# Four graph layers on 2708 nodes: queries, keys, values and outputs of a head as one run in DRAM

## The chip, the cores and the metric

The kernel runs on one core of a Trainium2 chip. The metric is device time in microseconds (us) from the start of the program to its end. A profile is one more execution, taken by the hardware profiler. The core has TensorE (PE, with its weight loads as PEld), VectorE (DVE), ScalarE (ACT), GpSimd (POOL) and SyncE (SP), each with its own queue in program order, and 16 DMA engines. Nearly all plain DMAs of this kernel are issued from SP; gathers and scatters by index are issued from POOL.

## The reference, cut to what matters

Input are 2708 nodes with 128 features and a dense matrix `adj` of 2708 x 2708, in which about 4 entries of a row and the diagonal are not zero. Four layers each normalise x, apply a relu, and add their result to x. The change concerns layer 1, graph attention. Here h is the normalised x:

```python
q = (h @ Wq.T).reshape(d, n, heads)      # d = 128, n = 2708, heads = 8
k = (h @ Wk.T).reshape(d, n, heads)
v = (h @ Wv.T).reshape(d, n, heads)
a = einsum('dnh,dmh->dnm', q, k) * d**-0.5 + adj + adj
a = softmax(a, axis=2)
out = einsum('dnm,dmh->dnh', a, v).reshape(n, heads * d)
x = x + out @ Wo.T
```

The reshape doesn't split features into heads. h @ Wq.T has 2708 rows of 1024 numbers, which are read as one long list of 2708 * 128 groups of eight numbers. What the kernel calls head d (there are 128) is groups d*2708 to d*2708 + 2707 of that list; node n of head d comes from row (d*2708 + n) // 128 of the projection. Layer 0 before and layers 2 and 3 after use the same `adj` and are not changed.

## The kernel before, in words

**Projection** (L620 to L655). Six chunks of up to 512 nodes; for each of the three weights and each of eight elements e one matmul with 128 weight columns stationary and up to 512 columns of hT moving, 144 in all. ACT and DVE in turn copy a result to every 25th element of a tile `qkv`, which is stored to `qkv_c`, laid out [128 groups of a row][node rows][25]: 8 of q, 8 of k, 8 of v and a one. Beside this, `in_order` (L560) sorts the lists of neighbours; its 22 scatters `list_d` (L612) on POOL each wait for the one before.

**The loop over heads** (L1258 to L1321). For each of 128 heads it goes six rounds. The softmax is split: without `adj` the exponential is a polynomial, evaluated by `keys`, `queries`, `moments`, `turn` and `evaluate` for all pairs of nodes; the few pairs with an `adj` entry are corrected apart. Nodes are spread over partitions as node t*128+p on partition p, t from 0 to 21, so that the last tile t = 21 has 20 rows only. `prepare` (L787) loads four heads (a group; there are 32) from `qkv_c` to `raw`, with `from_heads` (L545), which needs one or two DMAs a head. Queries are transposed by PE (L1226), ACT copies them (`fT`, L1228), and PE multiplies (L1238).

**Beside the loop** generators are advanced by a pace of 1.5 steps a round: first `by_node` (L829) loads each group once more (`n_raw`, three buffers), ACT copies it so that eight heads of a node are adjacent (`n_kv` two buffers, `n_q` one buffer), and for every pair of groups SP stores `kv_n` in pieces of 512 bytes and `q_n` in pieces of 256 bytes. Then `sorted_rows`, then `from_neighbours` (L891), which gathers `kv_n` rows of each node's neighbours and scatters corrections to `more_n`. When these are done, two steps a round go to `normalise` (L1033) and `project_out` (L669). A group's polynomial sums were stored to `o_g` by `sums` (L821); `normalise` loads them and the corrections, adds them on POOL, divides on DVE and stores outputs to `o_c` with `to_heads` (L550). `project_out` loads a tile of nodes as [groups][nodes][8], and multiplies eight times with a stationary operand of every eighth element. Generators yield a number of rounds to wait (`LOAD, SOON = 4, 2`). `begin` and `step` (L1089, L1108) choose what is advanced.

**Order.** The whole loop is in an order written out by hand (`manual_schedule`), so each engine's queue has its instructions as the source lists them. After the loop bounds are computed (L1325 to L1366), and what is left beside it is finished. If a bound failed, dense attention would be computed by loops L1423 to L1500; on these inputs these loops run zero times.

Of the kernel before, what the change touches and what calls it, by code (L numbers as in the profile page):

```python
# [45 lines left out]
def gnn4_kernel(  # L46
# [211 lines left out]
    with ExitStack() as ph:  # L258
# [9 lines left out]
        def by_head(src, name):  # L268

            nat = ap.tile([P, KC, C], FP, name=f"{name}_nat", tag="a_nat")  # L270
            nc.sync.dma_start(nat, src.rearrange("(t p) c -> p t c", p=P))
            dst = bp.tile([P, HEAD, C], FP, name=name)
            for i0, iw in _cuts(KC, 4):
                pt = ps.tile([P, BK], FP, name="w_ps", tag="tr")
                for i in range(iw):
                    nc.tensor.transpose(pt[:, i * P : (i + 1) * P], nat[:, i0 + i], ident)
                c0, cw = i0 * P // HEAD, iw * P // HEAD
                nc.vector.tensor_copy(
                    dst[:, :, c0 : c0 + cw],
                    pt[:, : iw * P].rearrange("p (c h) -> p h c", h=HEAD),  # L280
                )
            return dst
# [35 lines left out]
        with tc.manual_schedule():  # L318
# [3 lines left out]
            wT = [by_head(w, f"wT{i}") for i, w in enumerate((wq, wk, wv))]  # L322
# [207 lines left out]
    qkv_c = dram.tile([P, N + 1, QKV], FP, name="qkv_c")  # L530
    o_c = dram.tile([P, N, HEAD], FP, name="o_c")
# [6 lines left out]
    def runs(d, t0, n=P):  # L538

        sh, r = d * N % P, d * N // P + t0  # L540
        if sh + n <= P:
            return [(0, n, sh, r)]
        return [(0, P - sh, sh, r), (P - sh, n, 0, r + 1)]

    def from_heads(eng, dst, src, d, t0, nt, n=P):  # L545

        for p0, p1, c, r in runs(d, t0, n):
            eng.dma_start(dst[p0:p1], src[c : c + p1 - p0, r : r + nt])

    def to_heads(eng, dst, src, d, t0, nt, n=P):  # L550
        for p0, p1, c, r in runs(d, t0, n):
            eng.dma_start(dst[c : c + p1 - p0, r : r + nt], src[p0:p1])
# [67 lines left out]
    with ExitStack() as ph:  # L620
# [6 lines left out]
        zero = lp.tile([P, QKV], FP, name="zero")  # L627
        nc.gpsimd.memset(zero, 0.0)
        nc.sync.dma_start(qkv_c[:, N], zero)
        with tc.manual_schedule():  # L630
            ots = [op.tile([P, BK, QKV], FP, name=f"qkv{i}") for i in range(2)]
# [4 lines left out]
            for c, (c0, cw) in enumerate(cols):  # L636
                ot = ots[c % 2]
                for i in range(3):
                    for e in range(HEAD):
                        pq = pm.tile([P, BK], FP, name="qkv_ps", tag="mm")  # L640
                        nc.tensor.matmul(
                            pq[:, :cw], wT[i][:, e], hT[:, c0 : c0 + cw], start=True, stop=True
                        )
                        scale = (C**-0.5, 1.0, 1.0)[i]
                        to = ot[:, :cw, i * HEAD + e]
                        n += 1
                        if n % 2:
                            nc.scalar.mul(to, pq[:, :cw], scale)
                        else:
                            nc.vector.tensor_scalar_mul(to, pq[:, :cw], scale)  # L650
                            next(sort, None)
                nc.sync.dma_start(qkv_c[:, c0 : c0 + cw], ot[:, :cw])
# [4 lines left out]
    def load_wo(lp, wk_pool, ps, tag):  # L657
        wo_nat = wk_pool.tile([P, HD], FP, name="wo_nat", tag=tag)
        nc.sync.dma_start(wo_nat, wo)
        wo_h = wo_nat.rearrange("p (c k) -> p k c", k=HEAD)  # L660
        woT = lp.tile([P, HEAD, C], FP, name="woT")
        for k0, kw in _cuts(HEAD, 4):
            pt = ps.tile([P, 4, C], FP, name="wo_ps", tag="tr")
            for k in range(kw):
                nc.tensor.transpose(pt[:, k], wo_h[:, k0 + k], ident)
# [3 lines left out]
    def project_out(op, tag, bank, woT, t):  # L669
        r0, sz = rows[t]  # L670
        o = op.tile([P, P, HEAD], FP, name="o_cr", tag=tag)
        nc.sync.dma_start(o[:, :sz], o_c[:, r0 : r0 + sz])
        yield LOAD
        po = bank(t)
        for k in range(HEAD):
            nc.tensor.matmul(
                po[:sz], o[:, :sz, k], woT[:, k], start=k == 0, stop=k == HEAD - 1
            )
        yield SOON
        nc.vector.tensor_tensor(x_sb[:sz, t], x_sb[:sz, t], po[:sz], ALU.add)  # L680

    LOAD, SOON = 4, 2
# [3 lines left out]
    with ExitStack() as ph:  # L686
# [100 lines left out]
        def prepare(g, got):  # L787

            raw = kp.tile([P, GRP, NT, QKV], FP, name="raw")
            for i in range(GRP):  # L790
                from_heads(nc.sync, raw[:, i], qkv_c, g * GRP + i, 0, NT)
            for _ in range(8):
                yield
            for e, at in enumerate((q_at, k_at)):
# [11 lines left out]
            nc.vector.reduce_sum(  # L806
                part, v[:, :, :NF].rearrange("p i t k -> p i k t"), axis=AX.X
            )
# [4 lines left out]
            nc.tensor.matmul(to, ones, flat, start=True, stop=not REM)  # L813
            if REM:
                nc.tensor.matmul(to, ones[:REM], v[:REM, :, NF], start=False, stop=True)
# [13 lines left out]
        def by_node():  # L829
# [3 lines left out]
            def load(j):  # L833
                raws[j] = big.tile([P, GRP, NT, QKV], FP, name="n_raw", tag="big")
                for i in range(GRP):
                    from_heads(nc.sync, raws[j][:, i], qkv_c, j * GRP + i, 0, NT)
# [4 lines left out]
            for j in range(NG):  # L841
# [8 lines left out]
                for dst, src in (  # L850
# [4 lines left out]
                    nc.scalar.copy(dst, raw[:, :, :, src].rearrange("p i t k -> p t i k"))  # L855
                    yield
                    yield
                if j % 2:
                    hs = slice((j - 1) * GRP, (j + 1) * GRP)
                    store_rows(  # L860
# [4 lines left out]
                    store_rows(  # L865
# [167 lines left out]
        def normalise(g, ring):  # L1033

            if ring == "tm":
                ro = tm.tile([P, NT, GRP, VW], FP, name="r_raw", tag="tmp")
                co = tm.tile([P, NT, GRP, VW], FP, name="r_more", tag="c_q")
            else:
                both = big.tile([P, 2, NT, GRP, VW], FP, name="r_both", tag="big")
                ro, co = both[:, 0], both[:, 1]  # L1040
            nc.sync.dma_start(ro.rearrange("p t i k -> p (t i k)"), o_g[g])
            nc.sync.dma_start(
                co.rearrange("p t i k -> p t (i k)"),
                more_n[:, g * GRP : (g + 1) * GRP].rearrange("(t p) i k -> p t (i k)", p=P),
            )
            yield LOAD
            nc.gpsimd.tensor_tensor(ro, ro, co, ALU.add)
            yield SOON
            rs = sm.tile([P, NT, GRP], FP, name="r_rs")
            on = lp.tile([P, GRP, NT, HEAD], FP, name="r_on", tag="n_kv", bufs=2)  # L1050
# [7 lines left out]
            for t0, nt, sz in ((0, NF, P), (NF, 1, REM)):  # L1058
                for i in range(GRP if sz else 0):
                    to_heads(nc.sync, o_c, on[:sz, i, t0 : t0 + nt], g * GRP + i, t0, nt, sz)  # L1060
# [18 lines left out]
        rings = {"tm": [], "big": []}  # L1079
        room = {"tm": 2, "big": 3}  # L1080
        banks = []

        def bank(t):

            if not banks:
                banks.append(ps_v.tile([P, 2, BK], FP, name="v_ps"))
            return banks[0][:, t % 2, :C]

        def begin(summed):  # L1089

            if not beside or beside[0][1] >= summed:
                return None
            i, need, norm = beside[0]
            if not norm and any(e[2] <= need for e in under_way):
                return None
            for ring in ("tm", "big") if norm else ("big",):
                if len(rings[ring]) < room[ring]:
                    beside.pop(0)
                    gen = (
                        normalise(i, ring) if norm else project_out(big, "big", bank, woT, i)  # L1100
                    )
# [50 lines left out]
        got = []  # L1152
        fks, ys, fqs, fts, pms, mws, ros = {}, {}, {}, {}, {}, {}, {}
# [40 lines left out]
        def moments(d, h, n0, n1):  # L1194
# [3 lines left out]
            for t in range(*parts[h])[n0:n1]:  # L1198
                sz, m = rows[t][1], t - parts[h][0]
                nc.tensor.matmul(  # L1200
                    pms[d][:, :P],
                    fks[d][:sz, t],
                    ys[d, h][:sz, m * VW * B_ALL : m * VW * B_ALL + P],
# [53 lines left out]

        with tc.manual_schedule():  # L1258
# [20 lines left out]
            for d in range(D):  # L1279
                asked = queries(d + 1) if d + 1 < D else iter(())  # L1280
                for c in range(NCH):
# [31 lines left out]
                    if first is None:  # L1313
                        owed = 0
                        for _ in range(2):
                            step(n, max(d // GRP - 1, 0))
                g = d // GRP
                if d % GRP == GRP - 1:
# [6 lines left out]
            nc.vector.memset(top, 0.0)  # L1325
            p2 = sm.tile([C, 2], FP, name="p2")
            for e in range(2):
                pt = ps_t.tile([P, BK], FP, name="g_tr", tag="tr")
                nc.tensor.transpose(pt[:C, :P], most2[:, e], ident)
                nc.vector.tensor_reduce(p2[:, e : e + 1], pt[:C, :P], axis=AX.X, op=ALU.max)  # L1330
            nc.vector.tensor_tensor(top[:, 0:1], p2[:, 0:1], p2[:, 1:2], ALU.mult)
            nc.vector.tensor_tensor(top[:, 1:2], p2[:, 0:1], p2[:, 1:2], ALU.max)
            nc.vector.tensor_reduce(top[:, 2:3], nval, axis=AX.XY, op=ALU.max)
            nc.vector.tensor_reduce(top[:, 3:4], nval, axis=AX.XY, op=ALU.min)
            low = sm.tile([P, 1], FP, name="low")
            nc.vector.tensor_scalar_mul(top[:, 3:4], top[:, 3:4], -1.0)
            nc.vector.tensor_reduce(low, below, axis=AX.X, op=ALU.max)
            nc.vector.tensor_tensor(top[:, 3:4], top[:, 3:4], low, ALU.max)
            nc.vector.tensor_tensor(top[:, 3:4], top[:, 3:4], full, ALU.max)
            nc.vector.tensor_reduce(low, eighth, axis=AX.X, op=ALU.max)  # L1340
            nc.vector.tensor_tensor(top[:, 3:4], top[:, 3:4], low, ALU.max)
            pt = ps_t.tile([P, BK], FP, name="g_tr", tag="tr")
            nc.tensor.transpose(pt[:4, :P], top, ident)
            t4 = sm.tile([4, 1], FP, name="top4")
            nc.vector.tensor_reduce(t4, pt[:4, :P], axis=AX.X, op=ALU.max)
# [427 lines left out]
```

## Time and profile before

| | |
|---|---|
| median of 3 runs | 3328.97 us (3327.44 to 3329.23) |
| profiled execution | 3354.19 us, its span 3352.4 us |
| PE busy | 2691.7 us, 80% of the span |
| PE weight loads | 2273.0 us, 68% |
| DVE busy | 2202.7 us, 66% |
| ACT busy | 1314.8 us, 39% |
| POOL busy | 2009.3 us, 60% |
| DMA moved | 462.08 MB, mean 138 GB/s |
| packets under 512 B, of all | 159,650 of 312,741 |
| mean granted clock of TensorE | 0.89 |

The page gives busy times over the whole span, but the kernel is a sequence of stages with different limits, so shares of the span say little; the prediction cuts it into stages. A group of instructions is shown as line, engine, operation, tiles out<-in, count, then busy time and the mean of one in ns, and after the next bar the engine's idle time ahead of them. A wait is shown as "engine line <- whom it waited for: us in total, times, longest". In a table of stretches, DMA share is the mean busy share of the 16 DMA engines, so that 0.25 is four engines' worth.

### The profile page before, as it was taken

Reading aid. Unit: us, or ns where it says so; the run is one execution under the profiler, and the core shown is the slowest. Engines: PE = TensorE matmul, PEld = TensorE weight load, DVE = VectorE, ACT = ScalarE, POOL = GpSimd, SP = SyncE. Lnnn points to the kernel's source line nnn. Section 1 sums busy time; section 2 is a strip of 40 time slices with the busy share of each in tenths; the row PEclk is TensorE's granted clock in tenths of the full one; section 3 lists DMA queues with packets and bytes.
Section 4 is the critical chain, followed back from the end, with each engine's and each line's share of the span. In section 5 each row is a group of like instructions: output and inputs, shape, how many; then the busy total and the mean of one; then the engine's idle time right before and its main releaser. Section 6 shows DMA issues by size and latency. Waiting matters only on the chain. (4 is left out here: it accounts for less than half of the span.)

```text
span 3352.4 us, 50866 instructions
## 1 busy us (share of the span) xinstructions
PE 2691.7 (80%) x17781; PEld 2273.0 (68%) x17781; DVE 2202.7 (66%) x5135; ACT 1314.8 (39%) x3127; POOL 2009.3 (60%) x2263
## 2 busy tenths in 40 slices
PE   6477884888789999999999999999888897796044
PEld 4476543777788887888888788877777886443033
DVE  3868753666678888888888788887666675213222
ACT  3485462555544444444444444444322232102010
POOL 0111115555588888888988888889656663000775
PEclk6688896999999999999999999999888999895565
DMA  3452274777743333333334333343465712541322
GB/s 113 175 227 93 76 326 128 208 214 206 211 131 114 125 125 127 128 132 128 119 138 139 126 141 125 137 143 121 94 148 143 166 48 64 193 176 56 106 83 61
DMA packets 312741, 462.08 MB, mean 138 GB/s; under 512 B 159650, under 2 KB 234404, under 8 KB 289330
## 3 DMA queue, kind: packets, MB, share of 16 engines
q1 hardware_dynamic: 280870, 289.79, 28.3%
q0 software_dynamic: 31600, 168.86, 14.7%
q8 instruction: 148, 2.42, 0.3%
q14 instruction: 123, 1.01, 0.1%
HBM read 344.89 MB, written 113.67 MB: 137 GB/s over the span
## 5 line engine op out<-in xcount | busy, mean ns | idle before, releaser
L1238 PE MATMUL g_ps<-mw,fT 128*128 128x128 f32 x5632 | 817.5, 287 | 155.2 <-ACT fT L1228 115.1
L1238 PEld LDWEIGHTS g_ps<-mw,fT 128*128 128x128 f32 x5632 | 715.4, 196 | 290.6 <-ACT fT L1228 178.4
L1228 ACT COPY fT<-f_ps 128x512 f32<-128x512 f32 (+1 forms) x768 | 420.6, 548 | 1216.7 <-PE f_ps L1226 1216.6
L1200 PE MATMUL m_ps<-y,fk 128*128 128x128 f32 (+1 forms) x5632 | 768.2, 280 | 0.0
L1200 PEld LDWEIGHTS m_ps<-y,fk 128*128 128x128 f32 (+1 forms) x5632 | 699.9, 194 | 15.4
L1150 POOL TENSOR_TENSOR y<-bk,raw 128x792 f32<-128x792 f32 x256 | 415.8, 1624 | 432.1 <-ACT y L1181 420.3
L1246 DVE TENSOR_TENSOR z<-g_ps,bq 128x324 f32<-128x324 f32 (+1 forms) x768 | 355.6, 463 | 435.0 <-PE g_ps L1238 433.6
L1226 PE MATMUL f_ps<-ident,fq 128*128 128x128 f32 x2816 | 441.6, 276 | 14.4 <-DVE v_sum L817 9.3
L1252 DVE TENSOR_REDUCE o_raw<-z 128x36 f32<-128x324 f32 (+1 forms) x768 | 355.8, 463 | 26.4
L1150 POOL TENSOR_TENSOR fk<-bk,raw 128x352 f32<-128x352 f32 (+1 forms) x384 | 357.7, 955 | 0.1
L1226 PEld LDWEIGHTS f_ps<-ident,fq 128*128 128x128 f32 x2816 | 340.2, 144 | 16.2 <-DVE v_sum L817 10.6
L1150 POOL TENSOR_TENSOR fk<-raw,bk 128x352 f32<-128x352 f32 (+1 forms) x512 | 312.6, 640 | 3.1 <-ACT bk L719 2.3
L1147 DVE TENSOR_TENSOR fq<-bq,kq_ps 128x528 f32<-128x528 f32 (+1 forms) x512 | 288.2, 605 | 0.0
L930 POOL TENSOR_TENSOR c_z<-c_kv,c_q 128x1024 f32<-128x1024 f32 (+1 forms) x121 | 284.2, 2349 | 2.2 <-DMA c_kv<-kv_n,srt 1.4
L971 PE MATMUL v_ps<-c_v,ident 128*128 128x512 f32 (+1 forms) x484 | 233.3, 605 | 15.3 <-ACT c_acc L986 15.3
L1591 POOL DMA_INDIRECT g<-gate_d,srt x121 | 120.4, 995 | 110.2 <-issue 109.0
L1147 DVE TENSOR_TENSOR fq<-kq_ps,bq 128x352 f32<-128x352 f32 (+1 forms) x512 | 171.9, 378 | 0.0
L155 POOL CAST n_fl<-n_ci 128x40 f32<-128x40 int32 (+1 forms) x22 | 4.8, 218 | 251.9 <-DVE n_ci L138 251.9
L936 DVE TENSOR_REDUCE c_c<-c_z 128x128 f32<-128x1024 f32 (+1 forms) x121 | 147.5, 1219 | 3.4 <-POOL c_z L930 3.2
L954 DVE TENSOR_TENSOR c_v<-c_kv,c_c 128x1024 f32<-128x1024 f32 (+1 forms) x121 | 146.7, 1212 | 0.0
L971 PEld LDWEIGHTS v_ps<-c_v,ident 128*128 128x128 f32 (+1 forms) x484 | 82.0, 189 | 79.1 <-issue 58.8
L915 POOL DMA_INDIRECT c_kv<-kv_n,srt x121 | 117.8, 974 | 23.1 <-issue 9.6
(290 smaller groups left out, 3714.1 us busy)
## 6 DMA issues: line engine op xcount, KB each, us to landing
a_nat<-in_adj_dram SPq DMA_DIRECT2D x34, 1354.0 KB
qkv_c<-qkv SPq DMA_DIRECT2D x5, 6400.0 KB
a<-in_adj_dram SPq DMA_DIRECT2D x21, 1354.0 KB
kv_n<-n_kv SPq DMA_DIRECT2D x16, 1344.0 KB
o_g<-o_raw SPq DMA_DIRECT2D x32, 396.0 KB
q_n<-n_q SPq DMA_DIRECT2D x16, 672.0 KB
o_cr<-o_c SPq DMA_DIRECT2D x21, 512.0 KB
r_raw<-o_g SPq DMA_DIRECT2D x22, 396.0 KB
```

Of the source, the lines that this page charges most:

```text
L930: nc.gpsimd.tensor_tensor(zs[b][:sz], kvs[b][:sz, 0, :, 0], qs[t][:sz], ALU.mult)
L936: nc.vector.reduce_sum(cs[b][:sz], zs.pop(b)[:sz], axis=AX.X)
L954: nc.vector.tensor_tensor(z[:sz], kv[:sz, 0, :, 1].rearrange("p (j c) k -> p j c k", j=2), c.rearrange("p (j c) -> p j c", j=2)[:, :, :, None]
L971: nc.tensor.matmul(accs[t][:sz, j], ident[:sz, :sz], z[:sz, j].rearrange("p c k -> p (c k)"), start=s0 == 0, stop=s0 == ROOM[t] - 1,)
L1147: nc.vector.tensor_tensor(o, x, y, ALU.mult)
L1150: nc.gpsimd.tensor_tensor(o, x, y, ALU.mult)
L1200: nc.tensor.matmul(pms[d][:, :P], fks[d][:sz, t], ys[d, h][:sz, m * VW * B_ALL : m * VW * B_ALL + P], start=t == 0, stop=t == NT - 1,)
L1226: nc.tensor.transpose(pt[:, m], fqs[d][:, t0 + m], ident)
L1228: nc.scalar.copy(fts[d, c][:, :n], pt[:, :n])
L1238: nc.tensor.matmul(pg[:, m], ft[:, m], mws[d], start=True, stop=True,)
L1246: nc.vector.tensor_tensor(z[:, :n], pg[:, :n, : B_ALL * VW].rearrange("p t (k b) -> p t k b", k=VW), bqs[d % 2][:, t0 : t0 + n, None, :B_A ...
L1252: nc.vector.reduce_sum(ros[g][:, t0 : t0 + n, i], z[:, :n], axis=AX.X,)
```

## The change

All of layer 1 uses the flat order of the list. `qkv_d` has one row of 25 numbers for each of 2708 * 128 groups, `o_d` one row of 8, so that a head is one run of rows. A head's 2708 nodes are cut into 123 runs of 22 and a rest of two: node p*22+t lies on partition p, and partition 123 holds the rest. The other partitions of two fixed `raw` buffers are set to zero once, so `moments` and the sum of v use all 128 rows of every tile. Groups, per-node data and outputs are loaded and stored by one DMA for 123 partitions and a small one for the rest.

The projection goes by 22 tiles of nodes: hT stationary, 512 weight columns moving, six matmuls a tile, 132 in all, copied in runs of eight, with a store of 12,800 bytes a partition for each tile. The output projection loads whole rows of 1024 numbers, turns them by eight PE transposes, ACT copies them in two pieces, and eight matmuls follow later. `normalise` waits one more step before its store; the last group takes its sums from SBUF rather than from `o_g`. Spacing is `LOAD, SOON = 6, 2`; three steps a round are tried, and a group may begin earlier. The bounds are computed in small steps during the last three heads.

```diff
-    qkv_c = dram.tile([P, N + 1, QKV], FP, name="qkv_c")
-    o_c = dram.tile([P, N, HEAD], FP, name="o_c")
+    qkv_d = dram.tile([N * (P + 1), QKV], FP, name="qkv_d")
+    o_d = dram.tile([N * P, HEAD], FP, name="o_d")
...
+    WHOLE = N // NT
+    LEFT = N - WHOLE * NT
...
+    def group_of(src, g):
+
+        flat = src[g * GRP * N : (g + 1) * GRP * N].rearrange("(i n) k -> i n k", n=N)
+        return (
+            flat[:, : WHOLE * NT].rearrange("i (p t) k -> p i (t k)", t=NT),
+            flat[:, WHOLE * NT :].rearrange("(o i) n k -> o i (n k)", o=1),
+        )
+
+    def load_group(eng, dst, g):
+
+        main, rest = group_of(qkv_d, g)
+        eng.dma_start(dst[:WHOLE].rearrange("p i t k -> p i (t k)"), main)
+        eng.dma_start(
+            dst[WHOLE : WHOLE + 1, :, :LEFT].rearrange("p i t k -> p i (t k)"), rest
+        )
+
+    def store_group(eng, g, src):
+
+        main, rest = group_of(o_d, g)
+        eng.dma_start(main, src[:WHOLE].rearrange("p i t k -> p i (t k)"))
...
+    def store_nodes(eng, dst, src):
+
+        eng.dma_start(
+            dst[: WHOLE * NT].rearrange("(p t) k -> p t k", t=NT), src[:WHOLE]
+        )
+        eng.dma_start(
+            dst[WHOLE * NT :].rearrange("(o t) k -> o t k", o=1),
+            src[WHOLE : WHOLE + 1, :LEFT],
+        )
...
-            for c, (c0, cw) in enumerate(cols):
-                ot = ots[c % 2]
+            for t, (r0, sz) in enumerate(rows):
+                ot = ots[t % 3]
                 for i in range(3):
-                    for e in range(HEAD):
+                    scale = (C**-0.5, 1.0, 1.0)[i]
+                    for c0 in (0, HALF):
                         pq = pm.tile([P, BK], FP, name="qkv_ps", tag="mm")
                         nc.tensor.matmul(
-                            pq[:, :cw], wT[i][:, e], hT[:, c0 : c0 + cw], start=True, stop=True
+                            pq[:sz],
+                            hT[:, r0 : r0 + sz],
+                            wT[i][:, c0 * HEAD : (c0 + HALF) * HEAD],
+                            start=True,
+                            stop=True,
                         )
...
+        pt = turn_bank()
+        for k in range(KC):
+            nc.tensor.transpose(
+                pt[:, k // 4, (k % 4) * P : (k % 4) * P + sz],
+                nat[:sz, k * P : (k + 1) * P],
+                ident[:sz, :sz],
+            )
+        for j in range(KC // 4):
+            nc.scalar.copy(
+                oT[:, 4 * j : 4 * j + 4, :sz],
+                pt[:, j].rearrange("p (k c) -> p k c", k=4)[:, :, :sz],
+            )
+        yield SOON
+        add_sums()
+        po = sum_bank()
+        for k in range(KC):
             nc.tensor.matmul(
-                po[:sz], o[:, :sz, k], woT[:, k], start=k == 0, stop=k == HEAD - 1
-            )
+                po[:sz], oT[:, k, :sz], woT[:, k], start=k == 0, stop=k == KC - 1
+            )
...
-    LOAD, SOON = 4, 2
+    LOAD, SOON = 6, 2
...
-            raw = kp.tile([P, GRP, NT, QKV], FP, name="raw")
-            for i in range(GRP):
-                from_heads(nc.sync, raw[:, i], qkv_c, g * GRP + i, 0, NT)
+            raw = raws_g[g % 2]
+            load_group(nc.sync, raw, g)
...
-                for i in range(GRP):
-                    from_heads(nc.sync, raws[j][:, i], qkv_c, j * GRP + i, 0, NT)
+                main, _ = group_of(qkv_d, j)
+                nc.sync.dma_start(raws[j][:WHOLE].rearrange("p i t k -> p i (t k)"), main)
...
-                    store_rows(
+                    store_nodes(
                         nc.sync,
                         kv_n[:, hs].rearrange("n i k -> n (i k)"),
                         kv.rearrange("p t j i e k -> p t (j i e k)"),
                     )
...
+        raws_g = [lp.tile([P, GRP, NT, QKV], FP, name=f"raw{i}") for i in range(2)]
+        for b in raws_g:
+            nc.gpsimd.memset(b, 0.0)
...
-                    fks[d][:sz, t],
-                    ys[d, h][:sz, m * VW * B_ALL : m * VW * B_ALL + P],
+                    fks[d][:, t],
+                    ys[d, h][:, m * VW * B_ALL : m * VW * B_ALL + P],
...
-                        for _ in range(2):
-                            step(n, max(d // GRP - 1, 0))
+                        for _ in range(3):
+                            step(n, max((d - 1) // GRP, 0))
+                    if d >= D - 3:
+                        next(limits, None)
                 g = d // GRP
-                if d % GRP == GRP - 1:
+                if d % GRP == GRP - 1 and g < NG - 1:
                     sums(g, ros.pop(g))
```

## The prediction

> **What bounds the kernel now.** I read the page's slices first, then cut the span into stages at the lines that begin and end them: layer 0 to 379 us, projection of queries, keys and values to 497, start-up of the attention loop to 563, the loop to 2828, its tail to 2866, layers 2 and 3. The stage table (busy time of each engine, granted clock, DMA share, GB/s):
>
> ```profile
> core 0: us, PE busy (x) PEld busy (x) DVE busy (x) ACT busy (x) POOL busy (x), PEclk, DMA share, GB/s
> 379.00:497.00 118.00, 114.12 (x293) 53.52 (x292) 79.31 (x103) 73.18 (x73) 17.10 (x19) 0.97 0.60 253
> 497.00:563.00 66.00, 12.28 (x62) 10.93 (x62) 11.72 (x41) 6.50 (x20) 27.64 (x38) 0.53 0.52 173
> 563.00:953.00 390.00, 325.07 (x2554) 305.54 (x2554) 254.11 (x613) 214.38 (x478) 224.53 (x304) 0.93 0.70 191
> 953.00:2386.00 1433.00, 1338.51 (x9664) 1154.56 (x9665) 1177.39 (x2537) 622.93 (x1677) 1246.30 (x1304) 0.99 0.37 128
> 2386.00:2828.00 442.00, 372.68 (x2712) 353.65 (x2711) 288.35 (x643) 133.78 (x346) 261.43 (x276) 0.93 0.49 114
> 2828.00:2866.00 38.00, 16.60 (x75) 14.51 (x73) 10.02 (x38) 0.00 (x0) 5.70 (x4) 0.64 0.45 119
> ```
>
> TensorE fills the projection and the loop's middle. The stage 563 to 953 is another: beside the loop, `by_node` rewrites everything per node, and DMA is at 0.70. The waits of that stage already show the loop held by a store, because ACT takes its work in order:
>
> ```profile
> ACT n_q L855 <- DMA q_n<-n_q: 31.7, 5, 8.3
> ```
>
> So I looked at how fast single transfers go there. Three narrow windows: 607.0 to 608.5, in which only the load issued at 604.3 still moves (163.3 KB, that is 76 rows of 2200 B), then a kv_n store (512 B pieces, 128 partitions), then a q_n store (256 B pieces):
>
> ```profile
> 607.00:608.50 1.50, 1.50 (x16) 1.50 (x15) 0.85 (x2) 0.77 (x2) 0.00 (x0) 1.00 0.26 100
> 609.00:613.00 4.00, 3.27 (x26) 2.79 (x25) 1.69 (x5) 2.57 (x5) 0.43 (x1) 1.00 1.03 290
> 614.00:616.80 2.80, 1.78 (x16) 1.59 (x16) 1.58 (x5) 1.72 (x6) 2.80 (x7) 1.00 0.96 217
> ```
>
> The last two columns: the 76-row load runs on a quarter of the 16 DMA engines, 4, at 100 GB/s; the 128-row stores on all. Per engine: 25 GB/s at 2200 B, 18.1 at 512 B, 13.6 at 256 B.
>
> [...] 76 = 4x19 gets 4. [...] the q_n store, issued at 611.4, moves only when the kv_n store is through, near 613.6. [...]
>
> **The change, part by part.**
>
> *By-node stores and loads.* Node p*22+t on partition p fills 123 partitions; 123 = 3x41. [...] No row of this trace shows 3 engines; I take the per-engine rates above. A group's load is 1.082 MB at 75 GB/s, 14.4 us; a pair's kv_n store 1.385 MB at 54.4, 25.5 us; its q_n store 0.693 MB at 40.7, 17.0 us. Before, the two stores took 4.8 and 3.2 us at 290 and 217 GB/s. The second, small DMA of each (1 partition or 2 nodes) is nothing in bytes.
>
> [...] their times add: a pair of groups costs 2x14.4 + 25.5 + 17.0 = 71.3 us. The loop passes a pair in 12 yields at 1.5 a round, 8 rounds; before, the first and last kv_n stores are issued at 583.7 and 928.3, 23 us a pair. The query copy has one buffer, so ACT stops at the next pair's copy until q_n has landed; behind it in ACT's queue are the feature copies and fT, and so PE, DVE and POOL stop. The stores of a pair are issued some 14 us after ACT resumes (5.3 rounds), while the ring still has two loads, 27 us: it never runs empty and the stage takes its sum: 32 node loads 461, 16 kv_n 408, 16 q_n 272, 7 loads of `prepare` that fall in it 101, the rest about 10: 1252 us.
>
> *Start.* Projection: 132 matmuls of 512 columns for 120 of 512 and 24 of 148: 67,584 columns for 64,992, at 114.12/64,992 us each 118.7: it ends at 498, not 494. Evictions write runs of 8 and stay under it. Then:
>
> ```profile
> POOL list_d L612 <- DMA list_d<-rec,s_at: 99.3, 20, 8.9
> DVE W L780 <- DMA list_d<-rec,s_at: 28.6, 1, 28.6
> ```
>
> 22 scatters run one after another and end only at 539, each behind stores whose rows of 51,200 B hold an engine 2 us at 25 GB/s. Rows of 12,800 B hold it 0.5 us: I expect the scatters done near 500. The first load now waits for them, and for new memsets of its buffer on POOL behind nine others, about 9 us (estimate: the bk memset of 638 columns takes 0.64 us here; the two raw buffers have 2200 each): near 513, against 511 before. It lands near 529; before, its reader stood until 539 for the scatters. The first evaluation comes near 551 for 563. If the scatters are not faster, all moves 37 us later.
>
> *Together:* ring from 513 for 1252, then 15 us empty before the last pair's stores and 1.5 us to land: about 1782 for the first gather, which is at 955 in this trace. **+827**, and up to 30 for gaps between transfers, of which I take 10.
>
> *The loop's middle.* Loads of `prepare` take 14.4 us, but are issued 37 us before their first reader (1010.6 to 1047.7): hidden; with 23 us of lead gone they would stall 14 us a group. The last tile's moments now have 128 rows:
>
> ```profile
> L1200 PE MATMUL m_ps<-y,fk 128*128 128x128 f32 x5376 | 715.3, 278 | 0.0
> L1200 PE MATMUL m_ps<-y,fk 20*128 20x128 f32 x256 | 61.9, 321 | 0.0
> ```
>
> 242 ns busy a record against 133: 28 us of TensorE, 23 outside the stage that DMA now sets[...]. I take **-12** (0 to -23); the dropped 20-row v_t matmul is in it, and v_part's one more tile in 22 on DVE (1.6 us) is hidden.
>
> *The late part,* 2386 to 2828:
>
> ```profile
> PE v_ps L676 <- DMA o_cr<-o_c: 31.0, 11, 9.3
> PE g_ps L1238 <- DVE z L1246: 10.2, 2, 6.7
> PEld v_ps L676 <- DMA o_cr<-o_c: 10.0, 6, 4.8
> ```
>
> Some 40 us in which TensorE waits inside the loop for outputs just stored. Longer spacing (6 rounds for 4, one more step before the store) should take most away; but a group's store, 0.35 MB on 3 engines at some 20 GB/s each, takes 6 us. TensorE work of the output projection: 176 transposes at 441.6/2816 = 0.157 us and 352 passes at 817.5/5632 = 0.145: 79 for 85.7. ACT gets 44 copies of 0.58 = 26 us at 30% busy, hidden. DVE's bound tests move under the last three heads: hidden. I take **-28** (0 to -50).
>
> *The tail,* 38 us: the last group skips its trip through o_g, but SP has, in order, the flag reads, group 30's store, a tile's load, group 31's store and two loads, each waiting for the one before: about 32, **-6** (+8 to -14).
>
> Sum against this execution: 3352 + 837 - 12 - 28 - 6 = 4143. This execution (3354 us, span 3352) lies 24 us over the median of the runs (3329); I carry that over: **about 4120 us**.
>
> **Rivals.** (a) *Not slower:* the transfers spread after all, or stay hidden. It decides where a pair's ring work fits in 23 us: 71.3x3/k <= 23, from k = 10 engines. Then only the rest counts: 3329 - 12 - 46 = about 3270. For it: before, the same bytes were nearly hidden. Against: the 0.26 share above. (b) *Only loads are narrow:* if the DRAM side alone decided, 2706 = 11x246, stores on 11 engines cost 7.0 and 4.6 us; the ring sums to 461 + 101 + 186 + 10 = 758, first gather near 1288, +333: about 3620. (c) *The ring runs dry:* every pair adds a latency, 15 us by copies that wait for a late load of the same ring, 16 times, +240: about 4360. The clock drop after each stall speaks for it, the 13 us of slack against.
>
> **How the numbers follow.** The forecast has 0.80, (a) 0.05, (b) 0.06, (c) 0.09. Unknowns of the forecast: rates (-50 to +60), gaps (-10 to +20), scatters (-10 to +37), the three gains (+54 down to -41). Its own range is 4020 to 4260; to keep 8 in 10 with part of (c) I say 3980 to 4290. Under 0.2% (7 us) a measurement of this kernel tells nothing; faster 0.05, same 0.01, slower 0.94.
>
> **What would show it.** After: kv_n stores 70 to 76 us apart for 23, and every third pair 85 or more; ACT n_q waiting for q_n some 50 us, about 15 times; DMA share near 0.2 and 55 to 75 GB/s in a loop stage that ends near 1780; then heads of 17 us as before; list_d done near 500. Wrong if kv_n stores stay under 30 us apart, if the share there is over 0.5, or if the time is under 3900.

## The result

| | before | after |
|---|---|---|
| median of 4 runs | 3329.1 us (3327.4 to 3333.2) | 4042.6 us (4038.7 to 4053.8) |
| profiled execution, span | 3354.2 us, 3352.4 | 4038.7 us, 4036.9 |
| PE busy | 2691.7 us, 80% | 2680.9 us, 66% |
| mean granted clock | 0.89 | 0.82 |

The kernel is slower by 21.5%: ratio 1.2146, 95% interval 1.212 to 1.2173. The forecast was 4120 us, with a range of 3980 to 4290. TensorE has 11 us less to do, and stands idle for 695 us more of the span.

First the slices of the page, 101 us each:

```profile
PEclk6788965766666666899999999999998898979565
DMA  3632712222222222333434343434433545234232
GB/s 113 234 141 84 299 67 65 74 65 73 67 72 68 71 68 65 102 121 125 131 128 131 130 136 130 142 130 143 145 122 89 124 121 132 70 133 178 83 95 78
```

From slice 6 to 16 DMA moves 65 to 74 GB/s at two tenths (one tenth in slice 6). Cut into stages (busy times, clock, DMA share, GB/s):

```profile
core 0: us, PE busy (x) PEld busy (x) DVE busy (x) ACT busy (x) POOL busy (x), PEclk, DMA share, GB/s
...
550.00:1662.00 1112.00, 368.74 (x2551) 352.32 (x2552) 258.20 (x614) 217.20 (x487) 226.57 (x306) 0.67 0.21 68
...
3096.00:3546.00 450.00, 339.07 (x2718) 324.34 (x2717) 273.23 (x627) 143.97 (x358) 237.98 (x252) 0.91 0.44 110
3546.00:3584.00 38.00, 19.30 (x97) 15.99 (x97) 8.82 (x29) 5.56 (x19) 2.04 (x2) 0.69 0.28 102
```

The first row has the work of the stage of 390 us before (2551 matmuls for 2554), in 1112 us, at a DMA share of 0.21 for 0.70: some 3.4 engines of 16 for 11. The share runs somewhat over the true count (the 128-row kv_n store before shows 1.03 of 16), so it fits three engines. The waits of the whole span show who passes the delay on:

```profile
DVE z L1328 <- PE g_ps L1320: 1058.8, 316, 44.8
PEld g_ps L1320 <- ACT fT L1310: 841.0, 286, 44.4
...
ACT n_q L908 <- DMA q_n<-n_q: 617.9, 15, 44.3
```

Read from the bottom: ACT stands 41 us at each of 15 copies of queries, until the store before has landed; PE stands as long each time for ACT's `fT` behind it, DVE for PE. In this stage alone PE's own wait for `fT` is 718 us, for 60 in the same stage before. Last, three narrow windows in the transfers of one pair of groups. In the first only the kv_n store moves, in the second the q_n store, in the third a load:

```profile
669.00:686.00 17.00, 0.00 (x0) 0.00 (x0) 0.00 (x0) 0.00 (x0) 0.00 (x0) 0.50 0.22 65
690.00:700.00 10.00, 0.00 (x0) 0.00 (x0) 0.00 (x0) 0.00 (x0) 0.00 (x0) 0.50 0.24 54
703.00:715.00 12.00, 9.46 (x68) 9.04 (x69) 4.79 (x13) 7.09 (x18) 5.11 (x6) 0.85 0.20 76
```

All five engines stand still in both store windows, and TensorE's clock is at 0.50. At 65, 54 and 76 GB/s a kv_n store takes 1.385 MB/65 = 21.3 us, a q_n store 12.8, a group's load 14.2.

Where the time went, by the same events in both traces:

| stretch | before, us | after, us | difference | forecast |
|---|---|---|---|---|
| start to the first evaluation | 563.0 | 550.2 | -12.8 | -12 |
| start to the first gather (the row above is part of it) | 955.2 | 1662.4 | +707.2 | +837 |
| first to last gather (middle) | 1377.8 | 1350.6 | -27.2 | -12 |
| last gather to last evaluation (late part) | 495.3 | 533.0 | +37.7 | -28 |
| last evaluation to last sum (tail) | 37.7 | 26.9 | -10.8 | -6 |
| last sum to the end | 486.4 | 464.0 | -22.4 | 0 |

The last row is layers 2 and 3, which the change leaves alone. Its 22 us are in the gathers of layer 3 of the one profiled execution before, which lies 25 us over its median: this stretch took 486 us there and 463 to 467 in the profiles of all other runs, one with the old layout among them. The profile after lies 4 us under its median. So the medians, 713.5 us apart, differ by more than the spans, 684.5.

### The profile page after: what moved, and what is told of

Read it like the earlier page. It is cut to its first block, busy times and chain, and to the rows that moved or that the text cites. A ratio compares the mean times of both kernels' runs of the same rounds, so it can differ in the third digit from the quotient of the medians.

```text
span 4036.9 us, 49910 instructions
## 1 busy us (share of the span) xinstructions
PE 2680.9 (66%) x17869; PEld 2284.9 (57%) x17869; DVE 2181.6 (54%) x5129; ACT 1303.1 (32%) x3165; POOL 2008.0 (50%) x2266
## 3 DMA queue, kind: packets, MB, share of 16 engines
q1 hardware_dynamic: 268323, 286.42, 21.8%
## 5 line engine op out<-in xcount | busy, mean ns | idle before, releaser
L1320 PE MATMUL g_ps<-mw,fT 128*128 128x128 f32 x5632 | 833.3, 292 | 846.7 <-ACT fT L1310 780.7
L1320 PEld LDWEIGHTS g_ps<-mw,fT 128*128 128x128 f32 x5632 | 742.9, 202 | 968.0 <-ACT fT L1310 841.0
L1282 PE MATMUL m_ps<-y,fk 128*128 128x128 f32 x5632 | 763.8, 282 | 0.0
L1282 PEld LDWEIGHTS m_ps<-y,fk 128*128 128x128 f32 x5632 | 711.7, 200 | 0.2 <-issue 0.2
L1308 PE MATMUL f_ps<-ident,fq 128*128 128x128 f32 x2816 | 451.5, 281 | 10.2 <-DVE fq L1226 4.7
L1308 PEld LDWEIGHTS f_ps<-ident,fq 128*128 128x128 f32 x2816 | 348.6, 146 | 12.6 <-DVE v_sum L863 6.4
L908 ACT COPY n_q<-n_raw 124x704 f32<-124x704 f32 x32 | 26.3, 823 | 617.9 <-DMA q_n<-n_q 617.9
L1229 POOL TENSOR_TENSOR bk<-raw 128x88 f32<-128x88 f32 x384 | 124.5, 351 | 15.2 <-DMA raw<-qkv_d 15.2
```

Of the source, the lines that this page charges most:

```text
L1229: nc.gpsimd.tensor_tensor(o, x, y, ALU.mult)
L1282: nc.tensor.matmul(pms[d][:, :P], fks[d][:, t], ys[d, h][:, m * VW * B_ALL : m * VW * B_ALL + P], start=t == 0, stop=t == NT - 1,)
L1308: nc.tensor.transpose(pt[:, m], fqs[d][:, t0 + m], ident)
L1320: nc.tensor.matmul(pg[:, m], ft[:, m], mws[d], start=True, stop=True,)
```

## The experiments

The theory: every transfer of 123 partitions runs on 3 of 16 DMA engines (a DMA share of 0.20 to 0.24 in the windows above). All of these transfers are issued from SP, stand in one ring and move one after the other: in the kernel before, DMA still moved the kv_n store's 289 to 290 GB/s from 611.4 to 612.6 us, though a q_n store was issued at 611.4, and the q_n store's 217 only from 614. The ring's work then sets the stage up to the first gather. Rivals: the layout and the later stores cost by themselves; the latency of the store that ACT waits for (one `n_q` buffer) sets the pace, not the ring's throughput; only loads, or only stores, matter.

**1. All wide.** In each of these DMAs the partitions are cut in two:

```diff
+    CUT = 112
...
-        eng.dma_start(dst[:WHOLE].rearrange("p i t k -> p i (t k)"), main)
+        for p0, p1 in ((0, CUT), (CUT, WHOLE)):
+            eng.dma_start(dst[p0:p1].rearrange("p i t k -> p i (t k)"), main[p0:p1])
```

and likewise in `store_group`, `store_nodes` and `by_node`'s load.

> The changed kernel, with every transfer of 123 partitions (node loads, prepare's loads, the kv_n, q_n and o_d stores) issued as one of 112 and one of 11 partitions. Theory (three engines are the whole of the loss): a pair of groups needs about 2x2.9 + 4.8 + 3.2 + 1 = 15 us of the ring, less than the 23 us at which the loop passes a pair, so the first gather comes near 945 and the kernel takes 3250 to 3320 us: 3329 - 13 at the start - 27 in the middle - 11 in the tail, and in the late part between +38 (what after shows) and -28 (forecast). Rival (the contiguous layout, its transposed output projection or the later stores cost by themselves): over 3400. Rival (the single n_q buffer, that is the latency of a store and not its width): kv_n stores still over 40 us apart, over 3600.

Measured: 3207.9 us, 0.962 of the kernel before (0.9604 to 0.9636), faster than both kernels. First gather at 912; kv_n stores 21.7 us apart on average for 68.2. The stage:

```profile
541.00:912.00 371.00, 314.94 (x2559) 300.80 (x2560) 255.13 (x616) 216.90 (x486) 227.59 (x306) 0.95 0.80 197
```

Both rivals, over 3400 for the layout and over 3600 for the store's latency, are out. The width of the transfers is more than the whole loss: it costs 835 us, and the rest of the change gains 126 us, more than any side had expected: by the profiles against before, the first evaluation 22 us earlier, the stage up to the first gather another 21, the middle 31, the late part 36, the tail 16.

**2. Half wide.** Once only `store_nodes` is cut, once only the loads.

> Only the kv_n and q_n stores are split into 112 and 11 partitions; loads and o_d stores stay on three engines. Theory (times on the ring add): a pair needs 2x14.5 + 9 = 38 us, the stage 16x38 + 7x14.5 = 709 us instead of 1130, the first gather near 1232, the time near 3610 us (3560 to 3660). Rival (the stores alone make the loss, because ACT waits for q_n): the loads hide, below 3400. Rival (the loads alone): no change, near 4040.

> Only the node loads and prepare's loads are split into 112 and 11 partitions; stores stay on three engines. Theory (times on the ring add): a pair needs 2x2.9 + 21.2 + 12.7 = 40 us, the stage 16x40 + 7x2.9 = 660 us, the first gather near 1183, the time near 3565 us (3510 to 3620). Rival (the stores alone make the loss): near 4000. Rival (the loads alone): below 3400.

Measured: 3640.6 us (ratio 1.0917, 1.0899 to 1.0936) and 3642.1 us (1.0917, 1.0898 to 1.0935); kv_n stores 42.4 and 46.1 us apart; first gathers at 1257 and 1299. Neither half alone is the loss, as the theory has it: each saves some 400 us, and both together, with only the o_d stores left narrow (experiment 6), 783. But both times lie above what was expected, the second by 77 us and outside its range. With wide stores the period fits: 38 us a pair and, since five of `prepare`'s loads fall between the first and the last kv_n store, 4.7 a pair, 42.7 in all. The 25 us by which the first gather is late lie at the ends of the stage, where the ring is not full: the first kv_n store comes 81 us after the first load, whose four transfers take 57. With wide loads a rate was wrong. In windows of the run with wide loads, two loads together, then a kv_n and a q_n store:

```profile
830.00:837.00 7.00, 5.37 (x25) 5.37 (x26) 3.22 (x7) 4.88 (x13) 5.08 (x9) 0.50 1.04 259
842.00:860.00 18.00, 10.56 (x91) 9.94 (x89) 8.11 (x21) 6.27 (x16) 9.07 (x12) 0.94 0.21 65
864.00:873.50 9.50, 0.00 (x0) 0.00 (x0) 0.00 (x0) 0.00 (x0) 0.00 (x0) 0.50 0.24 54
```

Cut in two, the loads run at 259 GB/s in this window, not at 16 x 25: 4.2 us instead of 2.9. Then 2 x 4.2 + 21.3 + 12.8 + 1.4 for `prepare` = 43.9 us; 46.1 were measured. The other two are open. With 76, 65 and 54 GB/s the same sum gives 28.5 + 21.3 + 12.8 + 4.7 = 67.3 us for the changed kernel, and 68.2 were measured.

**3. Throughput or latency.** The order of the two stores of a pair is reversed (`q_n`, then `kv_n`), once with all narrow, once with all wide.

> The changed kernel, all still on three engines, with the order of the two stores of a pair reversed: q_n first, then kv_n. ACT, which waits for q_n, may go on one kv_n store (21 us) earlier. Theory (the ring's sum sets the pace, and the wait only hands it on): the bytes of the ring are the same and it never ran empty, so kv_n stores stay about 68 us apart on average and the time within 20 us of 4043. Rival (the latency of the store that ACT waits for sets the pace, as the single n_q buffer would have it): 15 times 21 us less, near 3725.

> All transfers wide and q_n stored ahead of kv_n. With wide transfers the ring is no longer full, and what is left of ACT's waits for q_n (22.8 us in 8 waits) is latency. Theory: these waits vanish, the time falls by about 20 us from 3208 to 3188 (3175 to 3200). Rival (the loop's own pace takes it back): 3200 to 3215.

Measured: narrow 4028.6 us (1.208, 1.2061 to 1.2099), 14 us less than the changed kernel, where the rival of latency had some 3725; wide 3204.6 us (0.96, 0.9575 to 0.9625). The waits of the narrow one:

```profile
ACT n_kv L908 <- DMA n_raw<-qkv_d: 336.4, 17, 24.2
ACT n_q L908 <- DMA q_n<-n_q: 293.1, 15, 23.2
```

In the changed kernel ACT waited 618 us for q_n and 44 for the next load; now it is 293 and 336. ACT goes on 21 us earlier, and stands nearly as much longer at the next load, which is behind kv_n in the ring. A wait names the last thing waited for; the pace is the ring's sum, and not the latency of one store. With all wide the waits for q_n fell from 22.8 to 13.1 us, but the time isn't told apart from 3207.9: that expectation missed.

**4. The mechanism in the kernel before.** Its kv_n and q_n stores, of 128 partitions, are issued as 123 and 5; nothing else is changed.

```diff
-                    store_rows(
+                    store_thin(
...
+    def store_thin(eng, dst, src):
+        for p0, p1 in ((0, 123), (123, P)):
+            eng.dma_start(
+                dst[: NF * P].rearrange("(t p) c -> p t c", p=P)[p0:p1], src[p0:p1, :NF]
+            )
+        eng.dma_start(dst[NF * P :], src[:REM, NF])
```

> The kernel before, with only its kv_n and q_n stores issued as one of 123 and one of 5 partitions of the 128 it writes. Theory: the width of the transfer is enough, without the new layout. A pair needs 33.9 us of stores [...]: 45 us, 16 times, and about 40 of prepare's loads: 760 us from 511, first gather near 1285, the time near 3660 us (3590 to 3720). Rival (it takes the new layout's merged rows or later loads as well): under 3400.

Measured: 3751.5 us (1.125, 1.1232 to 1.1269), first gather at 1370. Windows in a kv_n and a q_n store, and a wait of the stage from 563 to 1370:

```profile
782.00:796.00 14.00, 8.04 (x68) 7.47 (x66) 7.67 (x20) 4.09 (x11) 8.00 (x12) 0.95 0.22 65
803.00:811.00 8.00, 0.00 (x0) 0.00 (x0) 0.00 (x0) 0.00 (x0) 0.00 (x0) 0.50 0.24 54
```

```profile
ACT n_q L862 <- DMA q_n<-n_q: 417.7, 15, 34.2
```

The same rates, the same wait, and +418 us without the new layout, so the rival (under 3400) is out. It is 92 us more than expected, and outside the range: stores come 49.5 us apart, where 45 and about 2 of `prepare`'s loads were counted. Of the 45, 33.9 are stores at the measured rates; the other 11 are the author's estimate for the old loads by head, up to 16 DMAs a pair, and what these really add was not measured.

**5. How the width counts.** The cut of the first experiment is moved from 112 to 117, 115 and 119, so that nearly the same bytes go in the first piece.

> As the kernel with everything wide, but the 123 partitions are cut into 117 (9x13: nine engines) and 6 instead of 112 and 11. Rates per engine from the runs with three: 22 GB/s at 512 B, 18 at 256 B, 25 at 2200 B. A load is 4.6 + 0.35 us, a pair's stores 6.7 + 4.1 + 0.8; the loop passes a pair in 21.7 us when nothing stops it. Sum theory (the ring's work sets the pace as soon as it exceeds the loop's): 9.9 + 11.6 + 2.2 for prepare's loads = 23.7 us a pair, 16 times 2 more than with everything wide: about 3240 us. Chain theory (once loads are short, a pair takes what ACT needs from its query copy to the stores, 5.3 of 8 rounds or 14.4 us, and then the stores to their landing, 11.6 + 2): 28 us a pair, 16 times 6 more: about 3310 us (3280 to 3330). Rival (the number of engines does not matter above three): 3208.

> The same with a cut at 115 (5x23: five engines) and 8. A load is 8.1 + 0.35 us, a pair's stores 11.8 + 7.2 + 0.8. Sum theory: 16.9 + 19.8 + 3.7 = 40.4 us a pair. Chain theory: the two loads (16.9) outlast ACT's 14.4 us, so 16.9 + 19.8 + 2 = 38.7 to 42 us. Both: near 40 us a pair, 16 times 18 to 19 more than with everything wide, and 15 to 25 us more in the late part: 3520 us (3480 to 3560). Rival (what matters is 3 engines against many): under 3300.

> As the kernel with everything wide, but cut into 119 and 4 partitions. The run cut at 117 was expected with nine engines, but the largest divisor of 117 up to 16 is 13, and with 13 engines its 3216 us are what the sum gives (62.9 x 3/13 = 15 us a pair, under the loop's 21.7). 119 = 7x17 is seven engines, with two partitions more in the first piece. Theory (the divisor decides): a load is 6.0 + 0.35 us, a pair's stores 8.8 + 5.3 + 0.8, prepare's loads 2.8 a pair: 30.5 us (to 32 with landing), 15 times 9 to 10 more than with everything wide, 5 to 15 us more in the late part: 3355 us (3325 to 3385), about the kernel before. Rival (117 was fast because few engines already suffice once no transfer is on three): within 20 us of 3216.

| first piece | largest divisor up to 16 | kv_n stores apart, us | time, us | ratio to before (95%) |
|---|---|---|---|---|
| 112 | 16 | 21.7 | 3207.9 | 0.962 (0.9604 to 0.9636) |
| 117 | 13 | 21.8 | 3216.4 | 0.9645 (0.962 to 0.967) |
| 119 | 7 | 34.5 | 3423.6 | 1.0268 (1.0251 to 1.0285) |
| 115 | 5 | 41.8 | 3541.9 | 1.0621 (1.0595 to 1.0647) |
| 123 | 3 | 68.2 | 4042.6 | 1.2146 (1.212 to 1.2173) |

The order is that of the divisors, not of the sizes: two partitions more, 119 for 117, cost 207 us. The expectation at 117 was worked out for nine engines by mistake. Cut at 117, the kv_n and q_n stores still move at 255 and 193 GB/s, at DMA shares of 0.87 and 0.84, near 13 of 16 (0.81), and 8 us are lost. Whether 21.7 us is the loop's own pace, with no transfer in its way, isn't shown: with all wide the stage's DMA share is still 0.80, and ACT waits 22.8 us for q_n in it. At 115 the time is as expected, at 119 it is 69 us over the 3355 expected. Windows in a load, a kv_n and a q_n store of that run:

```profile
793.00:801.00 8.00, 8.00 (x46) 8.00 (x47) 4.05 (x9) 2.92 (x5) 1.62 (x1) 0.63 0.47 139
807.00:814.00 7.00, 5.97 (x52) 5.59 (x51) 5.52 (x15) 3.37 (x8) 6.71 (x10) 1.00 0.50 152
816.50:820.50 4.00, 0.00 (x0) 0.00 (x0) 0.00 (x0) 0.00 (x0) 0.00 (x0) 0.87 0.53 119
```

Over seven engines the stores keep close to 22 and 18 GB/s each (152/7 and 119/7), but the load has fallen from 25 to 20 (139/7): 7.8 us. 2 x 7.8 + 9.1 + 5.8 + 2.6 = 33.1 us a pair, for 34.5 measured and 30.5 forecast.

**6. The late part.** Only the o_d stores wide; and all wide but these.

> The changed kernel with only its o_d stores split into 112 and 11 partitions; node loads, prepare's loads, kv_n and q_n stores stay on three engines. Theory (the late part, from the last gather to the last evaluation, is slow because a projection waits for outputs that leave on three engines: 533 us in the changed kernel, 517 with wide loads, 459 with all wide): the late part falls to about 475 us and the time to about 3980 us (3960 to 4000), while the first gather stays near 1660. Rival (prepare's loads of 14.5 us stand ahead of everything in the same ring and hold the late part by themselves): the late part stays over 515, time over 4020. Rival (ACT's new copies in order, or three steps a round): no change, 4043.

> The reverse: everything wide (112 and 11 partitions) but the o_d stores, which stay on three engines. Theory: the late part is that of the run with wide loads alone, 517 us for 459, and the tail 27 for 22: 3208 + 57 + 5 = 3270 us (3250 to 3285). Rival (o_d stores are hidden once the loads are out of their way): within 10 us of 3208.

Measured: 3979.2 us (1.1937, 1.1914 to 1.196), late part 467 us; and 3259.3 us (0.9767, 0.9749 to 0.9785), late part 501. The waits of the late part in the changed kernel,

```profile
ACT o_both L718 <- PE v_ps L712: 77.3, 9, 21.4
PE v_ps L712 <- DMA o_both<-o_d: 50.7, 7, 17.9
...
ACT o_nat L718 <- PE v_ps L712: 28.5, 11, 16.1
```

and with all wide:

```profile
ACT o_both L723 <- PE v_ps L717: 19.0, 8, 3.4
...
ACT o_nat L723 <- PE v_ps L717: 10.5, 10, 1.6
```

and with only the o_d stores wide:

```profile
ACT o_both L721 <- PE v_ps L715: 34.5, 9, 10.0
...
PE v_ps L715 <- DMA o_both<-o_d: 11.2, 2, 6.5
```

PE waits at its transposes for rows that have just been stored; ACT waits for PE in order, with later `fT` copies behind it. The o_d stores alone are worth 63 us with the other transfers narrow and 51 with them wide. The narrow loads, which stand ahead in the ring, are small beside that: 467 us against 459 with all wide. The rivals, that these loads, the new ACT copies or the third step a round hold the late part by themselves, would have left it near 515 us or more.

**7. The last tile's 20 rows.** With all wide, the last tile's moments get 20 rows, as before the change.

```diff
-                    fks[d][:, t],
+                    fks[d][: 20 if t == NT - 1 else P, t],
```

(and the same rows of `ys`).

> As the kernel with everything wide, but the moments' matmuls of the last tile take 20 rows instead of 128, as the kernel before had them; the kernel leaves out the last tile's other nodes from the sums of every head. Theory for the loop's middle (27 us shorter where 12 were forecast): a record of 20 rows costs 321 ns and one of 128 rows 277 or less, and TensorE is the bound there, so it comes back by 19 us in the middle (442.2 + 38.2 against 461.4 us of moments), 22 to 28 in the whole loop: about 3232 us (3220 to 3240). Rival (the records of 20 rows hide in the pipeline, the gain was the dropped 20-row sum or the clock): within 8 us of 3208.

Measured: 3247.3 us (0.9735, 0.9719 to 0.9751), 39 us slower, and 7 over the end of the expected range. By the profiles 24 us are in the middle, 15 in the late part and 6 in the stage before the first gather. The middle is firm: it took 1345 to 1347 us in all other runs with wide loads. The 15 us of the late part are not: it took 459 us with all wide and 473 with all wide and the stores reversed, which is the same work there.

Groups of the whole middle, from the first to the last gather, with 20 rows:

```profile
L1328 PE MATMUL g_ps<-mw,fT 128*128 128x128 f32 x3498 | 498.5, 284 | 64.1 <-ACT fT L1318 33.3 <-DVE mw L1300 22.8 <-ACT kq_ps L1253 7.0
L1290 PE MATMUL m_ps<-y,fk 128*128 128x128 f32 x3348 | 440.9, 276 | 0.0
...
L1290 PE MATMUL m_ps<-y,fk 20*128 20x128 f32 x158 | 38.2, 321 | 0.0
```

and with all wide:

```profile
L1328 PE MATMUL g_ps<-mw,fT 128*128 128x128 f32 x3498 | 489.3, 281 | 69.5 <-ACT fT L1318 32.3 <-DVE mw L1300 23.4 <-ACT kq_ps L1253 12.9
L1290 PE MATMUL m_ps<-y,fk 128*128 128x128 f32 x3507 | 458.9, 276 | 0.0
```

The same number of moment matmuls (one record is missing) keeps TensorE busy 20 us longer with 20 rows in the last tile, and the evaluation 9 us longer. That covers the stretch's 24 us. So most of the middle's gain is these rows.

## Why the prediction was right, and where it was not

*Direction, mechanism and place* were right: three engines, for which the prediction had one load of 76 rows at a share of 0.26, are shown by the windows of 0.20 to 0.24 of 16, by the old kernel with 123 partitions (0.22 and 0.24) and by the cuts. That all transfers use the same three isn't shown, only that their times add, 67.3 us a pair for 68.2 measured. Also right: ACT waits 41 us 15 times where some 50 were forecast; kv_n stores are 64 us apart, and 79 where a load of `prepare` falls between (forecast: 70 to 76, 85 or more); 68 GB/s (55 to 75); scatters done at 507 (near 500), the first load at 514 (513).

*The term that was mis-sized* is the stores: 25.5 and 17.0 us, from 18.1 and 13.6 GB/s per engine, taken where 128-row stores ran on all 16. Three engines give 21.7 and 18. Sixteen stores of each were forecast at 408 + 272 us and take 341 + 205: 134 us less, while the loads (14.4 forecast, 14.2 measured) fit: their rate came from a transfer on 4 engines. That is the +837 that became +707. The prediction had noted the unknown rate, but put its size at 50 us to this side.

*Rival (a)* had its price too high: 3270 us for transfers that spread, where the wide kernel takes 3208. It left out the 21 us that the stage up to the first gather gains and 10 more at the start, and halved the middle. Whether these 31 us come from loading a group with few DMAs, where the old kernel needs one or two a head, no run tests. Its limit of 10 engines, an estimate from the ring's sum, isn't contradicted: 117 partitions (13 engines) lose 8 us, 119 (7) lose 216. *Rival (b)*, stores on 11 engines, is out: the stores moved at 65 and 54 GB/s. *Rival (c)*, a ring that runs dry, did not come about: the stage's DMA share of 0.21 is that inside single transfers (0.20 to 0.24), and the pace stayed when the stores were reversed. The clock did drop at the stalls: it was 0.50 in the windows where all stood still and from 704 to 706 us, when TensorE was busy throughout again, then 0.83 to 708 and 1.00 to 710.

*The start* came as forecast: POOL's waits for the scatters took 76.9 us for 99.3. That shorter rows hold an engine for less time was the author's estimate from the 25 GB/s of one load; no run shows how long a row holds one. *The middle* gained 27 us for 12: TensorE's busy time for the moments fell there from 442.0 + 38.2 to 461.4 us, and the dropped 20-row sum of v, which the forecast took as included, is another 8.1. The forecast had bounded it at 23 and halved that by estimate; with 20 rows the middle took 24 us more, the whole of the 23.

*The late part* failed in sign, +38 for -28. The step that failed is the one from "Longer spacing" to "takes 6 us": it priced the narrow store by itself and let the longer spacing cover it. It did not follow the tile's load, which stands behind these stores in the ring, and the new transposes and ACT copies, in order ahead of `fT`, that wait for it: 51 to 63 us for the narrow store. With only the o_d stores wide the late part gains 29 us, the forecast's size; with all wide, 36.

*The tail* gained 11 us for 6. *The offset*: the 24 us (25 by the runs' times) that the first profile lay over its median were rightly taken off; most were in layer 3 and are gone after.

So the forecast was too long by 837 - 707 = 130 us up to the first gather, 15 in the middle, 5 in the tail and 22 in layers 2 and 3, and too short by 66 in the late part. That leaves the 106 us between 4143 and the span of 4037. That 4120 came as near as 77 us to the 4043 measured is in part luck: the late part's error had the other sign.

## What to carry to other kernels

Before a layout is chosen, look for each large DMA at the largest number up to 16 that divides its partitions: the five widths tried here fell in that order, from 21.7 us a pair at 112 to 68.2 at 123. 123 partitions in one transfer cost 835 us, and the same bytes as 112 and 11 made the change worth 126 us. Where several transfers share a ring, add up the ring for one period of the loop (67.3 us here, 68.2 measured) and compare it with the period. The instruction that shows the wait may only pass it on: with the stores reversed, ACT's 618 us at one store became 293 there and 336 at a load, and the time fell by 14 us. Take the rate for few engines from a transfer on few engines, and the rate for many from one on many: here 21.7 and 18.1 GB/s each for the same store.

## What the runs showed of the hardware

No view names an engine; the count is read from shares and rates. The windows' DMA shares come to 3.2 to 3.8 of 16 engines at 123 partitions, 7.5 to 8.5 at 119, 13.4 and 13.9 at 117, and 15.4 and 16.5 for the stores of 128. The largest divisors up to 16, which are 3, 7, 13 and 16, lie within 1.5 engines of these; 119 partitions move 152 GB/s where 123 move 65, which is 7 to 3. For 112 and 115 partitions only the order of the times speaks, and for 112 a load at 1.04.

A DMA engine's rate fell when more of them moved. Per engine (the rate of a window like those above over this count):

| piece | 3 engines | 7 | 16 |
|---|---|---|---|
| store, 512 B | 21.7 GB/s | 21.7 | 18.1 |
| store, 256 B | 18.0 | 17.0 | 13.6 |
| load, 2200 B | 25.3 | 19.9 | 16.2 |

On 16 engines the 512-byte store moves 290 GB/s. The load's 259 is the mean of a window with two loads and their small second pieces, so that 16.2 may be low for the piece of 112 partitions alone. What limits the engines together was not tried. The old layout's 123-partition stores ran at the same 65 and 54 GB/s, so the order of the rows in DRAM is not what slows them.

In the changed kernel the DRAM side of the kv_n store is 2706 rows = 11 x 246, and only its SBUF side has the 123. On 11 engines its 65 GB/s would be under 6 an engine, where 16 gave 18.1 each.

A matmul record with 20 rows took 321 ns and one with 128 rows 276, and putting the 20 rows back made the kernel 39 us slower: the short tile was no saving at all.
